# A planned transformer-and-recurrence kernel: other planner prices, a recurrence in 32 chunks of 32 steps, output in 2 KB pieces

## The chip, the cores and the metric

The kernel runs on one core of a Trainium2 chip. The metric is the device time of one execution in microseconds (us), taken as the median of several runs. Engines are named as in the profile: PE is TensorE (matrix products; PEld are its weight loads), ACT is ScalarE (activations), DVE is VectorE, POOL is GpSimd, SP is SyncE, which here only issues transfers.

## The reference

The input x has 8 batch entries of 1024 tokens (64 x 16) with 128 channels, all in fp32. Three things are computed one after the other.

- Layer 0: eight heads of attention with scores over all 1024 tokens of the entry. The exponential of the scores is normalised over one token axis (64 values apart by 16), and the result is put through an exponential once more and normalised over the other axis (16 values). Then come the output product, a residual, a layer norm, a feed-forward part of 512 hidden units with relu, a residual and a layer norm.
- Layer 1, additive attention, with t the tokens and B their layer norm:

```
Wi     = B @ W.T
scores = sum_d v[d] * tanh(Wi[i, d] + Wi[j, d])      # 1024 x 1024 x 128 tanh per entry
t      = t + softmax(scores, axis=j) @ B
```

- Layer 1, recurrence: the layer norm of t times a weight, normalised over all entries and tokens (per channel), and then, from token to token of an entry, with y starting at zero:

```
y = sigmoid(wx[:, token] + y @ V.T);   t[token] += y
```

## The kernel before

**Planned part.** Function `fast_path` first loads weights and multiplies some of them together. Then all work of layer 0 and of the additive attention is put down as a list of operations of a `Plan` (lines 409 to 538): an operation has one engine or a choice of engines with a price in us each, the keys that it reads and writes, and a priority. `Plan.emit` is a list scheduler. It keeps a clock for each engine, takes the engine that can start first, and gives it, among the operations that could start within 0.15 us of that, the one with the best priority. An operation's inputs count as ready at the end of their producer plus that producer's `LATENCY`, or plus `AGAIN` where it ran on the same engine. The order that comes out is the order of the instructions on each engine; at run time each engine goes through its queue in order and waits on semaphores. Prices and latencies thus decide the order and some choices of engine, and nothing else.

Batch entries overlap: layer 0 of entry b + 1 is planned together with the additive attention of entry b. A pair of query tiles in layer 0 goes through scores (PE, L851), exponential (ACT, L854), sums and reciprocal (DVE, L858 and L859), division (DVE, L862), second exponential (ACT, L871), sums and reciprocal (DVE, L874 and L875), division (POOL, L885), transposes through PSUM (PE, L765; DVE, L777), the product with the values (PE, L899) and a sum (DVE, L906). The second attention makes groups of rows, four or more of them. A group is either done wholly on ACT, which adds by its bias (`tanh_row`, L994), or added on DVE (`add_row`, L998, or `add_rows`, L1004) or POOL (`add_rows`, L1004) into one of the `th` slots and put through one tanh on ACT (L1040). PE weighs the rows with v and collects them in the PSUM tile `sa` (L1057), and the slot comes free. Transposes and projections share two PSUM banks; `through_bank` (L755) takes a `Bank` and gives it back.

After the additive attention of an entry its tokens are parked in DRAM (L1205) in halves, and so is their projection wx (L1221).

**Tail.** When the plan is out, its SBUF is given up and the tail begins (lines 1325 to 1389). The statistics are put together, the parked tokens are fetched into `xr` (L1340), and the normalised wx is written as `ws`, one DVE instruction for each step number l (L1346). The recurrence is cut into `NCH` = 64 chunks of `LCH` = 16 tokens, which run side by side. To find each chunk's starting value, a first pass over 16 steps runs on the tokens of the chunk ahead of it, beginning at nothing; the second pass over 16 steps produces the output, so there are 32 steps. A step has two halves, of 32 chunks each and all 8 entries (256 columns): a product of the identity with `ws` (L1365), a product of the weight with the former y on top (L1367), a sigmoid on ACT (L1369), and, in the second pass, a copy on DVE into `ys` (L1374). In the first pass chunk 0 has no predecessor and is left out (`skip`); its y is cleared before the second pass (L1372). At the end 16 pieces of 4 tiles each are transposed (PE, L1382), added to `xr` (DVE, L1384) and sent out (L1386), by turns from the ACT and the SP queue, in rows of 512 B:

```
out=a["out"][b, 4 * g * P : 4 * (g + 1) * P, :].rearrange("(t p) c -> p t c", p=P), in_=ot
```

Of the kernel before, what the change touches and what calls it, by code (L numbers as in the profile page):

```python
# [9 lines left out]
F32 = mybir.dt.float32  # L10
# [388 lines left out]
class Bank:  # L399


    def __init__(self, *choice):
        self.choice = choice

    def __call__(self):
# [3 lines left out]
class Plan:  # L409
# [14 lines left out]

    LATENCY = {"PE": 0.12, "ACT": 0.08, "DVE": 0.08, "POOL": 0.15, "SP": 8.0}
    AGAIN = {"PE": 0.0, "ACT": 0.0, "DVE": 0.04, "POOL": 0.1, "SP": 8.0}

# [27 lines left out]
    def emit(self, slack=0.15, switch=0.1, stay=0.015):  # L455
# [26 lines left out]
        def start_at(n, t, e):  # L482
            take = ops[n][5]
            if take:
                t = max(t, min(bank_free.get(c[0], 0.0) for c in take.choice))
            if e == "POOL" or (e == "DVE" and ops[n][8]):
                t = max(t, port_free)
            return max(t, free[e])
# [20 lines left out]
        while any(open_.values()):  # L509
            first, e = min(  # L510
                (min(start_at(n, t, e) for n, t in open_[e]), i) for i, e in enumerate(engines) if open_[e]
            )
            assert first < never
            e = engines[e]
            n, start = min(
                ((n, s) for n, s in ((n, start_at(n, t, e)) for n, t in open_[e]) if s <= first + slack),
                key=lambda c: (ops[c[0]][2][0] + places[c[0]][e][1] + (stay if e == "PE" and ops[c[0]][3] != mode else 0), c[0]),
            )
            _, fn, _, m, _, take, give, _, port = ops[n]
            if take:  # L520
                take.name, take.tile = min(take.choice, key=lambda c: bank_free.get(c[0], 0.0))
                bank_free[take.name] = never
            cost = places[n][e][0]
            if e == "PE":
                if m != mode:
                    cost += switch
                mode = m
            free[e] = start + (cost if e != "SP" else 0.2)
            if e == "POOL" or (e == "DVE" and port):
                port_free = start + cost  # L530
            began[n], done[n], by[n] = start, start + cost, e
            for q in places[n]:
                open_[q] = [c for c in open_[q] if c[0] != n]
            if give:
                bank_free[give.name] = done[n] + self.LATENCY[e]
            self.order.append((n, e, start, done[n]))
            fn(e)
            finish(n)
# [22 lines left out]
def fast_path(ctx: ExitStack, tc: tile.TileContext, a: dict, fits):  # L561
# [12 lines left out]
    SCALE = 1.0 / math.sqrt(C)  # L574
    NCH = 64
    LCH = N // NCH
# [21 lines left out]

    parked = [tile_of(dram, f"parked{b}", [P, NT, C]) for b in range(NB)]

# [183 lines left out]
    def layer0(b):  # L784
# [16 lines left out]
        for n_part, part in enumerate(parts):  # L801
# [3 lines left out]
            for h in range(H):  # L805
# [18 lines left out]
                for s in () if alone and n_part else range(2):  # L824

                    def values(bank, h=h, s=s):
# [6 lines left out]
                    through_bank(  # L833
                        values, 0.95, [kx], copy(vp[:, 4 * s : 4 * s + 4, :]), evict(0.68), [], [kvp + (s,)], L0, banks
                    )
                for qt in qts:
# [11 lines left out]
                    def scores(_, sc=sc, u=u, qt=qt):  # L848
# [3 lines left out]

                    add(("PE", 1.74), scores, r=[kx, ("u", h % 2, qt // 4)], w=[kc], pri=L0)
                    add(("ACT", 0.98), lambda _, sc=sc: nc.scalar.activation(sc, sc, AF.Exp, scale=SCALE),  # L854
                        r=[kc], w=[kc], pri=L0)
# [7 lines left out]

                    add(("DVE", 1.49), first_sums, r=[kc], w=[k1], pri=L0)
                    add(("DVE", 1.22), divide, r=[kc, k1], w=[ke], pri=L0)
# [4 lines left out]
                    ks = [("e", pair, q) for q in range(2)]  # L870
                    add(("ACT", 1.9), lambda _, e2=e2: nc.scalar.activation(e2, e2, AF.Exp), r=ks, w=ks, pri=L0)  # L871

# [3 lines left out]

                    add(("DVE", 3.25), second_sums, r=ks, w=[k2], pri=L0)
                    na = next_aT()
                    aT = aTs[na]
                    for q in range(2):  # L880
# [7 lines left out]
                        for s in range(2):  # L888
                            through_bank(
                                transposes([e[:, t * P : (t + 1) * P] for t in range(4 * s, 4 * s + 4)]), 0.52, [ke],  # L890
                                copy(aT[:, 4 * s : 4 * s + 4, q * P : (q + 1) * P]), evict(0.68), [],
                                [("aT", na, q, s)], L0, banks,
# [15 lines left out]
                    for s in range(2):  # L908
                        add(
                            ("PE", 1.74), lambda _, attend=attend, s=s: attend(s),  # L910
                            r=[kvp + (p,) for p in range(2)] + [("aT", na, q, p) for q in range(2) for p in range(2)],
# [5 lines left out]
            for qh in range(2) if part is None else (part,):  # L917
                Xg, kg = X[:, 4 * qh : 4 * qh + 4, :], kX + (qh,)
                through_bank(
                    transposes([zs[:, t * P : (t + 1) * P] for t in range(4 * qh, 4 * qh + 4)]), 0.52, [kz + (qh,)],  # L920
                    copy(Xg), evict(0.68), [], [kg], L0, banks,
                )

                def affine1(Xg=Xg):
# [5 lines left out]
                through_bank(  # L930
                    transposes([Xg[:, i, :] for i in range(4)]), 0.52, [kg], copy(z1T), evict(0.68), [], [k1], L0, banks
                )
# [38 lines left out]
    def group(it, at0, r0, k, wiT, all_wi, L1, ROWS, fillers, chain, left, both, first_half):  # L971
# [30 lines left out]
        def add_rows(eng, c):  # L1002
# [8 lines left out]
        work = {  # L1011
            "ACT": [(0.18 + 0.833e-3 * (w - begin[c]), lambda c=c, r=r: tanh_row(c, r)) for c, r in each],
            "POOL": [
                (0.27 + 1.62e-3 * k * (w - begin[c]), lambda c=c: add_rows(nc.gpsimd, c)) for c in range(4)
            ],
            "DVE": [(0.30 + 1.04e-3 * (w - begin[c]), lambda c=c, r=r: add_row(c, r)) for c, r in each]
            if k < 4
# [35 lines left out]
        def times_v(_):  # L1053
# [14 lines left out]
        add(  # L1068
            ("PE", k * (1.69e-3 * (w - begin[0]) + 0.005 * n)), times_v, r=[("tanh", g)] + before,
            w=[("sa", it, r0)] + after, pri=L1, mode="groups", give=slot,  # L1070
# [101 lines left out]
    def attention(b, it, X, kX, B, kB, E_at, L1):  # L1172

        for j0 in range(it + 1, NT, 4):
# [3 lines left out]
                [("E", it, j) for j in js],  # L1178
                copy(ET[:, j0 - 1 : j0 - 1 + len(js), :]), ("DVE", 0.15 + 0.132 * len(js)), [],
                [("ET", j) for j in js], L1,  # L1180
# [19 lines left out]
        if it % 4 != 3:  # L1200
# [3 lines left out]
        add(  # L1204
            ("SP", 4.0), lambda _: nc.sync.dma_start(out=parked[b][:, 4 * qh : 4 * qh + 4, :], in_=Xg),  # L1205
            r=[kg], w=[("parked", b, qh)], pri=L1,
# [129 lines left out]

    ys = rn.tile([P, NB, N], F32, tag="ys", name="ys")
    xr = rn.tile([P, NB, NT, C], F32, tag="xr", name="xr")
    for b in range(NB):
        nc.sync.dma_start(out=xr[:, b], in_=parked[b])  # L1340
    steps = ys.rearrange("p b (c l) -> p c b l", l=LCH)

    ws = rn.tile([P, LCH, NCH, NB], F32, tag="ws", name="ws")
    for l in range(LCH):
        step = wx.rearrange("p b (c l) -> p l c b", l=LCH)[:, l]
        nc.vector.tensor_scalar(ws[:, l], step, sc, off, ALU.mult, ALU.add)  # L1346

    with tc.tile_pool(name="ps_w", bufs=2, space=PSUM) as ps_w, tc.tile_pool(
        name="ps_t", bufs=2, space=PSUM
    ) as ps_t:
        HC = NCH // 2
        prev = [None, None]
        for k in range(2 * LCH):
            l = k % LCH
            early = k < LCH
            for half in range(2):
                c0, c1 = half * HC, (half + 1) * HC  # L1360
                skip = 1 if early and half == 0 else 0
                src = ws[:, l, c0 + skip - early : c1 - early, :]
                acc = ps_w.tile([P, HC, NB], F32, tag=f"acc{half}", name=f"acc{half}")
                to = acc[:, skip:, :]
                nc.tensor.matmul(to, ident, src, start=True, stop=k == 0)  # L1365
                if k:
                    nc.tensor.matmul(to, vf_sb, prev[half][:, skip:, :], start=False, stop=True)  # L1367
                y = rn.tile([P, HC, NB], F32, tag=f"y{half}", name=f"y{half}", bufs=3)
                nc.scalar.activation(y[:, skip:, :], to, AF.Sigmoid)  # L1369
                if k == LCH - 1 and half == 0:  # L1370

                    nc.vector.memset(y[:, 0:1, :], 0.0)  # L1372
                if not early:
                    nc.vector.tensor_copy(steps[:, c0:c1, :, l], y)  # L1374
                prev[half] = y

        n = 0
        for g in range(NT // 4):
            for b in range(NB):
                pt = ps_t.tile([P, 4, C], F32, tag="yt", name="yt")  # L1380
                for i in range(4):
                    nc.tensor.transpose(pt[:, i, :], ys[:, b, (4 * g + i) * P : (4 * g + i + 1) * P], ident)  # L1382
                ot = rn.tile([P, 4, C], F32, tag="ot", name="ot", bufs=3)
                nc.vector.tensor_tensor(ot, pt, xr[:, b, 4 * g : 4 * g + 4, :], ALU.add)  # L1384
                eng = nc.sync if n % 2 else nc.scalar
                eng.dma_start(  # L1386
                    out=a["out"][b, 4 * g * P : 4 * (g + 1) * P, :].rearrange("(t p) c -> p t c", p=P), in_=ot
                )
                n += 1
# [67 lines left out]
```

## Time and profile before

| what | us |
|---|---|
| median of 3 runs (5790.97 to 5795.5) | 5794.7 |
| the profiled execution's own time | 5790.2 |
| its span, first to last instruction | 5788.3 |
| PE busy (modelled) | 5221.0 |
| ACT busy | 5282.6 |
| DVE busy | 4697.6 |
| POOL busy | 4218.7 |
| last instruction of the planned part on PE begins | 5702.9 |
| first product of the recurrence (L1365) | 5709.5 |
| last product of the recurrence (L1367) | 5765.1 |
| last add of the output (L1384) begins | 5782.6 |

Busy times are sums over one profiled execution; engines overlap. A group of the profile gives the source line, engine and operation, what is written from what, the shape and count, then the busy time and the mean of one instruction in ns, and then how long the engine stood idle before them and who released it. The lines of waits give total us, number and longest. The lines of a timeline give start, duration and how many instructions were merged. The clock is that of PE's array, as a share of its full rate. An fp32 product shows as two matmul instructions; a transpose as one.

### The profile page before, as it was taken

The numbers are of one execution on the slowest core, as the hardware profiler recorded it, in microseconds if no ns is written. First come the engines' busy times: TensorE is split into PE (matmuls) and PEld (weight loads), VectorE is DVE, ScalarE is ACT, GpSimd is POOL, SyncE is SP. The second block draws the span as 40 slices with busy tenths as digits, with TensorE's granted clock in tenths as the row PEclk, the third lists the DMA queues.
The fourth block names the chain that finished last, engine by engine and source line by source line (L and its number), as shares of the span: only waits on it lengthen the run. The fifth ranks groups of instructions, "written<-read, shape, count | busy, mean of one in ns | idle before, by whom it ended". The sixth has DMA issues, their size and how long they took to land.

```text
span 5788.3 us, 97417 instructions
## 1 busy us (share of the span) xinstructions
PE 5221.0 (90%) x38885; PEld 2783.0 (48%) x38885; DVE 4697.6 (81%) x7236; ACT 5282.6 (91%) x4978; POOL 4218.7 (73%) x2714
## 2 busy tenths in 40 slices
PE   8899999999889999899998998899998999986567
PEld 6555544555445455454554554444554454443125
DVE  7899766877897788977998788977889678898885
ACT  5489999999999999999998999999998999999993
POOL 2352798788788879798786887788796887863871
PEclk9999999999999999999999999999998999998998
DMA  2000000000000000000000000000000000000001
GB/s 59 1 4 1 1 1 5 7 3 1 1 5 8 1 1 5 5 5 1 1 5 5 5 1 1 5 8 1 1 1 3 6 1 1 1 26 8 1 1 63
DMA packets 27328, 37.79 MB, mean 7 GB/s; under 512 B 2464, under 2 KB 19232, under 8 KB 26864
## 3 DMA queue, kind: packets, MB, share of 16 engines
q1 hardware_dynamic: 21760, 27.99, 1.5%
q8 instruction: 307, 5.03, 0.4%
q10 hardware_dynamic: 4944, 3.16, 0.2%
q14 instruction: 157, 1.29, 0.1%
q0 software_dynamic: 160, 0.33, 0.0%
HBM read 19.41 MB, written 12.06 MB: 5 GB/s over the span
## 4 chain that ended last, share of the span: by engine, by line
PE 52%; DVE 23%; ACT 19%; issue 4%; POOL 2%; DMA 0%; DVEq 0%; ACTq 0%; POOLq 0%; SPq 0%
PE sa L1057 19%; PE m L899 11%; PE sc L851 9%; ACT th L1040 8%; ACT th L994 7%; PE m L765 6%; DVE aT L777 2%; DVE th L1004 2%; DVE th L998 2%; DVE stat_e L874 2%; DVE stat_e L858 2%; ACT wx L871 2%; ACT sc L854 2%; DVE wx L862 2%; DVE X L737 2%
## 5 line engine op out<-in xcount | busy, mean ns | idle before, releaser
L1004 POOL TENSOR_TENSOR th<-wiT 128x1024 f32<-128x1024 f32 (+52 forms) x2124 | 3167.8, 1526 | 405.9 <-PE sa L1057 337.5
L1057 PE MATMUL sa<-th,vpat 128*32 128x512 f32 (+33 forms) x24576 | 2121.8, 470 | 230.9 <-ACT th L1040 219.4
L994 ACT ACTIVATE th<-wiT 128x128 f32<-128x128 f32 (+60 forms) x3092 | 2231.2, 795 | 13.7 <-PE sa L1057 13.5
L1040 ACT ACTIVATE th<-th 128x2490 f32<-128x2490 f32 (+50 forms) x760 | 2069.4, 2745 | 98.9 <-DVE th L998 52.5
L885 POOL TENSOR_TENSOR wx<-wx,stat_e 128x1024 f32<-128x1024 f32 x512 | 992.5, 1959 | 862.2 <-DVE stat_e L875 600.9
L1057 PEld LDWEIGHTS sa<-th,vpat 128*32 128x32 f32 x24576 | 674.8, 112 | 1480.7 <-issue 854.4
L851 PE MATMUL sc<-xT,wx 128*128 128x512 f32 x2048 | 982.2, 604 | 24.8 <-DVE wx L862 23.4
L899 PE MATMUL m<-aT,wx 128*128 128x256 f32 x3584 | 883.1, 394 | 15.1 <-DVE aT L777 13.6
L899 PEld LDWEIGHTS m<-aT,wx 128*128 128x128 f32 x3584 | 668.6, 194 | 269.0 <-issue 112.8
L998 DVE TENSOR_SCALAR_CACHE_REDUCE th<-wiT 128x328 f32<-128x328 f32 (+36 forms) x960 | 681.0, 709 | 83.9 <-PE sa L1057 17.8
L858 DVE TENSOR_REDUCE stat_e<-sc 128x16 f32<-128x1024 f32 x512 | 620.5, 1212 | 154.1 <-ACT sc L854 153.0
L777 DVE COPY aT<-m 128x512 f32<-128x512 f32 x927 | 601.4, 676 | 168.7 <-PE m L765 165.1
L874 DVE TENSOR_REDUCE stat_e<-wx 128x128 f32<-128x2048 f32 x256 | 583.7, 2280 | 129.8 <-ACT wx L871 129.0
L765 PE MATMUL m<-ident,wx 128*128 128x128 f32 x3896 | 573.7, 283 | 80.4 <-DVE aT L777 47.0
L862 DVE TENSOR_TENSOR wx<-sc,stat_e 128x1024 f32<-128x1024 f32 x512 | 623.2, 1218 | 22.9 <-POOL wx L885 0.5
L765 PEld LDWEIGHTS m<-ident,wx 128*128 128x128 f32 x3896 | 432.4, 142 | 378.4 <-issue 175.2
L854 ACT ACTIVATE sc<-sc 128x1024 f32<-128x1024 f32 x512 | 513.4, 1005 | 96.6 <-PE sc L851 83.4
L871 ACT ACTIVATE wx<-wx 128x2048 f32<-128x2048 f32 x256 | 486.8, 1902 | 91.4 <-DVE wx L862 88.2
L851 PEld LDWEIGHTS sc<-xT,wx 128*128 128x128 f32 x2048 | 358.4, 192 | 353.2 <-issue 300.3
L1004 DVE TENSOR_TENSOR th<-wiT 128x1024 f32<-128x1024 f32 (+27 forms) x288 | 361.3, 1302 | 2.0 <-ACT th L994 1.1
L875 DVE RECIPROCAL stat_e<-stat_e 128x128 f32<-128x128 f32 x256 | 244.0, 953 | 8.8
L906 DVE TENSOR_TENSOR zs<-m,zs 128x256 f32<-128x256 f32 x212 | 86.0, 406 | 170.0 <-PE m L899 169.4
(168 smaller groups left out, 3040.6 us busy)
## 6 DMA issues: line engine op xcount, KB each, us to landing
xT<-in_xt_dram SPq DMA_DIRECT2D x8, 512.0 KB, 3.7
th<-in_x_dram SPq DMA_DIRECT2D x8, 512.0 KB, 7.0
parked<-X SPq DMA_DIRECT2D x16, 256.0 KB, 2.0
xr<-parked SPq DMA_DIRECT2D x8, 512.0 KB, 7.0
parked_wx<-bT SPq DMA_DIRECT2D x14, 256.0 KB, 2.0
wx<-parked_wx SPq DMA_DIRECT2D x7, 512.0 KB, 3.3
out_dram<-ot ACTq DMA_DIRECT2D x8, 256.0 KB, 2.4
out_dram<-ot SPq DMA_DIRECT2D x8, 256.0 KB, 2.4
```

Source lines behind the costliest of these rows:

```text
L765: nc.tensor.transpose(bank[:, i * P : (i + 1) * P], s, ident)
L777: nc.vector.tensor_copy(dst, src)
L851: nc.tensor.matmul(sc[:, cols], u[:, qt * P : (qt + 1) * P], xT[:, cols], start=True, stop=True)
L858: nc.vector.tensor_reduce(r1, sc.rearrange("p (m g) -> p g m", g=G), AX.X, ALU.add)
L862: nc.vector.tensor_tensor(e3, sc3, r1.unsqueeze(1).to_broadcast([P, M, G]), ALU.mult)
L885: nc.gpsimd.tensor_tensor(e3, e3, r2[:, q, :].unsqueeze(2).to_broadcast([P, M, G]), ALU.mult)
L899: nc.tensor.matmul(bank()[:, :256], vp[:, t, :], aT[:, t, :], start=t == 0, stop=t == NT - 1)
L994: nc.scalar.activation(rows(c)[:, r, :], wiT[:, i0 + begin[c] :], AF.Tanh, bias=w_i(c, r))
L998: nc.vector.tensor_scalar(rows(c)[:, r, :], wiT[:, i0 + begin[c] :], w_i(c, r), 0.0, ALU.add, ALU.add, accum_out=unused)
L1004: eng.tensor_tensor(rows(c), wiT[:, i0 + begin[c] :].unsqueeze(1).to_broadcast(shape), w_i(c).unsqueeze(2).to_broadcast(shape), ALU.add,)
L1040: lambda _: nc.scalar.activation(slot()[:, : at[4]], slot()[:, : at[4]], AF.Tanh),
L1057: nc.tensor.matmul(sa[32 * c : 32 * c + 32, s:s1], vpat[:, 31 - r0 - r : 63 - r0 - r], rows(c)[:, r, s - at0 - begin[c] : s1 - at0 - begin ...
```

## The change

There are four parts.

1. The planner's `LATENCY` and `AGAIN` get larger values, and prices of single operations change: scores, value products, exponentials, sums and copies are priced higher by 0.01 to 0.11 us, a DVE row lower at its fixed part (0.30 to 0.21), a times-v product at 0.03 instead of 0.005 a piece. The scheduler itself and the priorities stay.
2. `Bank` can hold a choice of its own for an engine (`own`, `of`). No caller gives one.
3. The recurrence: `NCH` is 32 and `LCH` 32. The first pass has `EARLY` = 16 steps, on the last 16 tokens of the chunk ahead, and the second pass 32, so 48 steps. The halves are now of 4 entries with all 32 chunks each (128 columns). `ws` is written in 32 instructions of 256 elements, in the order in which the steps use it. Chunk 0 is left out of the first pass in both halves, and both are cleared.
4. The output: a partition now holds eight consecutive tokens, so `ys` is laid out by token modulo 8, a piece is sent in rows of 2 KB, and the pieces go entry by entry. There are four `ot` buffers and four PSUM tiles for the transposes instead of three and two. The tokens are parked in plain token order, so a parked half is written in rows of 512 B instead of 2 KB; the fetch has 4 KB rows as before.

The diff, cut to its core:

```diff
-    LATENCY = {"PE": 0.12, "ACT": 0.08, "DVE": 0.08, "POOL": 0.15, "SP": 8.0}
-    AGAIN = {"PE": 0.0, "ACT": 0.0, "DVE": 0.04, "POOL": 0.1, "SP": 8.0}
+    LATENCY = {"PE": 0.28, "ACT": 0.2, "DVE": 0.15, "POOL": 0.3, "SP": 8.0}
+    AGAIN = {"PE": 0.0, "ACT": 0.0, "DVE": 0.08, "POOL": 0.15, "SP": 8.0}
...
-                t = max(t, min(bank_free.get(c[0], 0.0) for c in take.choice))
+                t = max(t, min(bank_free.get(c[0], 0.0) for c in take.of(e)))
...
-    NCH = 64
+    NCH = 32
...
-    parked = [tile_of(dram, f"parked{b}", [P, NT, C]) for b in range(NB)]
+    parked = [tile_of(dram, f"parked{b}", [N, C]) for b in range(NB)]
...
-                    add(("PE", 1.74), scores, r=[kx, ("u", h % 2, qt // 4)], w=[kc], pri=L0)
-                    add(("ACT", 0.98), lambda _, sc=sc: nc.scalar.activation(sc, sc, AF.Exp, scale=SCALE),
+                    add(("PE", 1.81), scores, r=[kx, ("u", h % 2, qt // 4)], w=[kc], pri=L0)
+                    add(("ACT", 1.02), lambda _, sc=sc: nc.scalar.activation(sc, sc, AF.Exp, scale=SCALE),
...
-                    add(("DVE", 1.49), first_sums, r=[kc], w=[k1], pri=L0)
+                    add(("DVE", 1.6), first_sums, r=[kc], w=[k1], pri=L0)
...
-            "ACT": [(0.18 + 0.833e-3 * (w - begin[c]), lambda c=c, r=r: tanh_row(c, r)) for c, r in each],
+            "ACT": [(0.19 + 0.833e-3 * (w - begin[c]), lambda c=c, r=r: tanh_row(c, r)) for c, r in each],
...
-            "DVE": [(0.30 + 1.04e-3 * (w - begin[c]), lambda c=c, r=r: add_row(c, r)) for c, r in each]
+            "DVE": [(0.21 + 1.05e-3 * (w - begin[c]), lambda c=c, r=r: add_row(c, r)) for c, r in each]
...
-            ("PE", k * (1.69e-3 * (w - begin[0]) + 0.005 * n)), times_v, r=[("tanh", g)] + before,
+            ("PE", k * (1.67e-3 * (w - begin[0]) + 0.03 * n)), times_v, r=[("tanh", g)] + before,
...
+    EARLY = 16
+    HB = NB // 2
+    ws = rn.tile([P, LCH, NB, NCH], F32, tag="ws", name="ws")
+    ys = rn.tile([P, NB, NT, NCH, LCH // NT], F32, tag="ys", name="ys")
+    steps = wx.rearrange("p b (c l) -> p l b c", l=LCH)
+    order = [LCH - EARLY + k for k in range(EARLY)] + list(range(LCH))
+    for l in order[:LCH]:
+        nc.vector.tensor_scalar(ws[:, l], steps[:, l], sc, off, ALU.mult, ALU.add)
...
+        for k, l in enumerate(order):
+            early = k < EARLY
+            skip = 1 if early else 0
             for half in range(2):
...
+                bs = slice(half * HB, (half + 1) * HB)
+                acc = ps_w.tile([P, HB, NCH], F32, tag=f"acc{half}", name=f"acc{half}")
+                to = acc[:, :, skip:]
+                nc.tensor.matmul(to, ident, ws[:, l, bs, 0 : NCH - skip], start=True, stop=k == 0)
                 if k:
...
+                    nc.tensor.matmul(to, vf_sb, prev[half][:, :, skip:], start=False, stop=True)
+                y = rn.tile([P, HB, NCH], F32, tag=f"y{half}", name=f"y{half}", bufs=3)
+                nc.scalar.activation(y[:, :, skip:], to, AF.Sigmoid)
...
-                    nc.vector.tensor_copy(steps[:, c0:c1, :, l], y)
+                    nc.vector.tensor_copy(ys[:, bs, l % NT, :, l // NT], y)
...
-                    out=a["out"][b, 4 * g * P : 4 * (g + 1) * P, :].rearrange("(t p) c -> p t c", p=P), in_=ot
+                    out=a["out"][b].rearrange("(p t) c -> p t c", t=NT)[:, 4 * g : 4 * g + 4, :], in_=ot
```

## The prediction, made before the result was known

> **What bounds the kernel now.** I read the page first (engines, slices), then the waits of ScalarE (ACT), then the busy time of stretches of the span, then the tail's groups and its timeline. From the page:
>
> ```profile
> span 5788.3 us, 97417 instructions
> PE 5221.0 (90%) x38885; PEld 2783.0 (48%) x38885; DVE 4697.6 (81%) x7236; ACT 5282.6 (91%) x4978; POOL 4218.7 (73%) x2714
> PE   8899999999889999899998998899998999986567
> ACT  5489999999999999999998999999998999999993
> ```
>
> ACT and PE are both busy nine tenths in every slice from the fourth to the thirty-fifth: in the planned part of the kernel these two bound together. The last slice is the tail (recurrence and output), where ACT has 3. Busy time by stretch, two batches in the middle and three stretches of the tail (us; then busy and count of PE, PEld, DVE, ACT, POOL; then TensorE clock, DMA share, GB/s):
>
> ```profile
> 1800.00:2470.00 670.00, 630.81 (x4831) 333.07 (x4827) 548.21 (x826) 638.93 (x556) 543.10 (x350) 0.98 0.01 3
> 2470.00:3130.00 660.00, 618.65 (x4696) 324.12 (x4695) 557.23 (x826) 621.71 (x534) 531.00 (x337) 0.98 0.01 4
> 5709.00:5713.00 4.00, 3.48 (x8) 2.86 (x9) 4.00 (x7) 1.93 (x3) 0.00 (x0) 0.50 1.01 398
> 5741.00:5766.50 25.50, 25.44 (x121) 22.20 (x120) 12.53 (x31) 11.24 (x30) 0.00 (x0) 1.00 0.00 1
> 5766.50:5788.30 21.80, 11.79 (x60) 7.87 (x58) 10.96 (x17) 0.00 (x0) 0.00 (x0) 0.77 0.69 196
> ```
>
> ACT idles 5% in the middle batches; the recurrence is all PE (25.44 of 25.50); the output stage is no engine's. Its groups:
>
> ```profile
> L1365 PE MATMUL acc<-ws,ident 128*128 128x256 f32 x96 | 29.5, 390 | 0.0
> L1369 ACT ACTIVATE y<-acc 128x256 f32<-128x256 f32 x48 | 18.4, 383 | 22.2 <-PE acc L1367 11.1 <-DVE ys L1374 11.0
> L1346 DVE TENSOR_SCALAR ws<-wx,scb,offb 128x512 f32<-128x512 f32 x16 | 11.1, 839 | 0.1
> L1384 DVE TENSOR_TENSOR ot<-yt,xr 128x512 f32<-128x512 f32 x16 | 11.0, 691 | 5.8 <-DMA out_dram<-ot 5.2 <-PE yt L1382 0.7
> ```
>
> The output adds wait 5.2 us for output transfers, because the three ot buffers are still being written out. The rest of the working rests on these lines of the timeline (start, length):
>
> ```profile
> 5695.00 1.95 PE L1186 MATMUL m<-B,E 128*128 128x129 f32 x16
> 5713.01 1.30 PE L1367 MATMUL acc<-y,vf_sb 128*128 128x248 f32 x4
> 5757.80 0.60 PE L1365 MATMUL acc<-ws,ident 128*128 128x256 f32 x2
> 5758.23 0.59 PE L1367 MATMUL acc<-y,vf_sb 128*128 128x256 f32 x2
> 5765.14 0.59 PE L1367 MATMUL acc<-y,vf_sb 128*128 128x256 f32 x2
> 5782.62 0.69 DVE L1384 TENSOR_TENSOR ot<-yt,xr 128x512 f32<-128x512 f32 x1 [0.68 <-DMA out_dram<-ot]
> ```
>
> and these of ACT's waits:
>
> ```profile
> ACT wx L871 <- DVE wx L862: 88.2, 50, 14.4
> ACT sc L854 <- PE sc L851: 83.4, 71, 6.0
> ACT th L1040 <- DVE th L998: 52.5, 31, 4.7
> ACT th L1040 <- DVE th L1004: 36.3, 21, 4.0
> ```
>
> and two of the page's groups, ACT rows and POOL rows of the tanh work:
>
> ```profile
> L1004 POOL TENSOR_TENSOR th<-wiT 128x1024 f32<-128x1024 f32 (+52 forms) x2124 | 3167.8, 1526 | 405.9 <-PE sa L1057 337.5
> L994 ACT ACTIVATE th<-wiT 128x128 f32<-128x128 f32 (+60 forms) x3092 | 2231.2, 795 | 13.7 <-PE sa L1057 13.5
> ```
>
> **What the Trainium skill says.** "TensorE: Matmul & The Clock Gate", Back-to-back issue gap, gives N/2.4 + 2.5 ns a matmul: 0.109 us for 256 columns. The trace disagrees for this fp32 form: 0.43 us for two (5757.80 to 5758.23), 0.215 each. I use the trace. The same page, What's actually happening, says that the array runs at half rate until about 3.4 us of activity; the trace agrees (clock 0.50 in 5709 to 5713, 1.00 from 5713.6 by the clock records). "DMA: Bandwidth & Descriptors", Why small descriptors are slow, says each packet carries a fixed cost; the trace agrees: packet records last 28.6 ns for the 512 B of the output and 84 ns for the 2 KB of the parked writes, so 16 engines carry 286 and 390 GB/s.
>
> **The change, part by part.**
>
> *Recurrence.* Before, 32 steps, each two halves of two products of 256 columns, two instructions a product: 8 x 0.215 = 1.72 us. From the first recurrent product (5713.01) to the last (5765.14): 52.1 us. After, 16 early and 32 late steps, halves of 128 columns (4 batches x 32 chunks). PE's spacing at this width: sixteen matmuls of 129 columns span 1.95 us, one alone lasts 0.275, so (1.95 - 0.275)/15 = 0.112 us; a step is 8 x 0.112 = 0.89 us. The chain through one half is the other limit: 0.112 + 0.275 for the product, 0.04 to ACT (5738.97 to 5739.01 in the records), a sigmoid of 128 elements (0.383 for 256, 1.007 for 1024, L854: slope 0.81 ns, so 0.28), about 0.04 back, and a weight load of about 0.11 ahead of the product, since the wait sits on the load: 0.86 us. So PE still ends last, narrowly: 47 steps x 0.90 = 42.3 us. The start is earlier: the first normalisation has 256 elements instead of 512 (0.15 + 1.04 ns each: 0.42 against 0.68), the first product is half as wide at the cold clock (0.21 instead of 0.41 us an instruction), and fewer cold products stand ahead of the first recurrent one: 5711.7 against 5713.0, -1.3 us. Against that, PE idles while the sigmoid table loads (1.28 us, at 5710.76 now), so it may stay at half rate one window longer: +1.7 us. Sum: 42.3 - 52.1 - 1.3 + 1.7 = -9.4 us; bounds -11 (warm at once) and 0 (a step of 1.09 us: another 0.2 us in the chain).
>
> *Normalisation and copies on DVE.* 32 x 0.42 = 13.4 us instead of 11.1, but a step needs one only each 0.9 us, and the first late copy comes after 16 steps, so it hides behind the recurrence. 64 copies of 128 elements (0.28 us) instead of 32 of 256 (0.42): 18 us in the 29 us of the late steps, hidden too. The second clearing of the first chunk is 0.07 us of DVE, ahead of its use. Uncovered, these would be 2.3, 4.5 and 0.1 us.
>
> *Output.* Now from the last recurrent product (5765.14) to the last add's end (5783.31) is 18.2 us. After: last copy 1.1 us behind the last product (shorter product, sigmoid, copy; 1.5 now), then 16 adds. With 2 KB packets 256 KB take 0.67 us, below the add's 0.69, and there are four ot and four PSUM buffers; so DVE paces it, 16 x 0.75 with its hand-over = 12.0, or PE's transposes where the clock is at half (4 x 0.22 = 0.9 a piece). I take 12.5: 13.6 us, -4.6; bounds -5.5 and -1. The last transfer lands in 2.0 us (parked, 2 KB) rather than 2.4 (out): -0.4.
>
> *Parked writes.* 16 writes now go in 512 B pieces: 256 KB in 0.92 instead of 0.67 us of the queues, at a DMA share of 0.01 to 0.02. Nothing waits for them until the reload at 5705.1; the last is issued at 5697.6, lands about 2.0 us later and then about 2.3. Cost 0; uncovered, 0.3.
>
> Tail together: -9.4 - 4.6 - 0.4 = -14.4; I take -13.5, a rounding towards the losses of hand-overs not seen.
>
> *The planner.* `own` is passed by no caller: nothing. The prices and latencies change the order of instructions on each engine up to 5700 us, not the work as such, apart from which engine adds rows. PE's prices rise by about 4% for scores and attend, ACT's by 1 to 4%, POOL's not at all; DVE's rise by 0.11 (first sums), 0.05 and 0.02, and fall by 0.09 for an added row. The trace's reading of these: first exponential 1.007 (0.98 to 1.02), first sums with reciprocal 1.215 + 0.253 = 1.47 (1.49 to 1.6), a row of 535 elements comes every 0.93 us on DVE (5655.06, 5655.99, 5656.92; before's price 0.86, after's 0.77), PE's result reaches ACT about 0.2 us after its priced end (a tail of 0.17 behind the last spacing, and 0.04; 0.12 to 0.28). So before's prices lie closer, after's are mostly cautious and one is too low. The trace cannot say what order results. What it gives is the scatter: the xT loads, one a batch, are issued at 955.0, 1640.7, 2307.8, 2983.3, 3668.6, apart by 685.7, 667.1, 675.5, 685.2 under one set of prices, a deviation of 9 us. Over seven batches and two schedules that is 9 x 2.65 x 1.41 = 34 us; milestones within a batch jitter and partly cancel, so I estimate 15 to 30. My likeliest value is 0.
>
> Sum on the profiled run (span 5788.3, time 5790.2): 5776.7. The median of the runs is 4.5 above that run: **5781**.
>
> **Rivals.** *B, caution covers waits.* The four waits shown are 260 us of ACT, in which the planner thought an input ready that was not. With latencies 0.07 to 0.16 longer it puts a row of tanh there instead. For: ACT bounds, and these waits are frequent and short (173, 1.5 us each). Against: much of such a wait is a late chain and not a hand-over, and PE is as full as ACT. If 15% go: -40, 5741.
>
> *C, rows move to ACT.* A group of four rows is either added on POOL or DVE and put through one tanh of ACT, or done on ACT in four (L994). By the records an L994 costs ACT 0.19 us beside its elements (0.284 less an overlap of 0.096), the single tanh 0.10: a group that moves to ACT costs the bound engine 4 x 0.19 - 0.10 = 0.65 us. Place: batches 1 to 6. With slots priced free 0.28 us after PE instead of 0.12 and POOL's hand-over at 0.30 instead of 0.15, the planner finds ACT free first more often. For: POOL already idles 337.5 us for slots that PE holds. Against: ACT's own prices rise, DVE's row gets cheaper. It decides from (13.5 + 11.6) / 0.65 = 39 groups, 5% of the 760 that go through one tanh now. At 9%, 68 x 0.65 = 44 us, or for any order as much worse: 5825. The cheap DVE row is a smaller case of the same sign: 353 rows in the last batch (5220 to 5677), each priced 0.085 us lower, are at most 30 us of work that the plan does not see, the first part of it free, as ACT waits for these rows only 12.4 us there.
>
> *D, the recurrence becomes a chain.* If a step is 1.05 instead of 0.90 us, 7 us of the gain are lost: 5788. It lies inside the likeliest case. That the change does nothing it says is excluded: widths and packet sizes are in the code.
>
> **How the numbers follow.** A (tail gain, planned part within 13 us of now): 0.45, 5781, own range 5768 to 5794. B: 0.30, 5741, reaching from 5710 to 5768. C and other worse orders: 0.25, 5825, from 5794 to 5855. 0.2% of 5794.7 is 11.6 us, about what a measurement here can tell from no change: bounds 5783.1 and 5806.3. Faster: 0.27 of A and all of B, 0.57; same: 0.18 of A and 0.05 of C, 0.23; slower 0.20. The range leaves a third of B below 5738 and some 0.1 of C above 5822.
>
> **What would show it.** Right: the recurrence's matmuls of 128 columns at 0.11 us, a step of 0.9, last add some 14 us after the last recurrent product without waits for output transfers, the tail after the last projection 13 us shorter; the four waits of ACT summing to about 260 again. B: that sum clearly under 220. C: over 3250 of the L994 (3092 now, four to eight a group), or ACT waiting for DVE rows over 35 us after 5220. Wrong altogether: the span up to the tail moved by more than 45 us either way, or a step above 1.1 us.

## The result and the profile after

The changed kernel takes 5802.0 us (median, 5797.8 to 5808.4) against 5791.9 us for the kernel before in the same comparison: ratio 1.0016, 95% interval 1.0009 to 1.0023. It is slower by a sixth of a per cent, where 0.24% faster was forecast. The new tail gives nearly what was expected of it, and the planned part takes more than that back.

The page of the changed kernel; line numbers are higher by 5 to 7 in the planned part and by up to 14 in the tail:

```profile
span 5799.4 us, 97823 instructions
PE 5211.0 (90%) x39013; PEld 2774.9 (48%) x39013; DVE 4749.4 (82%) x7487; ACT 5268.3 (91%) x4948; POOL 4210.9 (73%) x2702
PE   8899999899998999999998999989998998997567
ACT  5489999999997999999999999979998799999994
```

Both kernels end the planned part with the same stretch of work, which begins with an exponential of 640 columns into E. By the timelines, before and then after:

```profile
5677.07 0.70 ACT L1153 ACTIVATE E<-sa 128x640 f32<-128x640 f32 x1 [2.07 <-PE sa L1057]
5702.32 0.70 ACT L1158 ACTIVATE E<-sa 128x640 f32<-128x640 f32 x1 [2.07 <-PE sa L1062]
```

So the planned part is 25.3 us longer. From there to the end it is 111.2 us before and 97.0 after: the tail is 14.2 us shorter. 25.3 - 14.2 = 11.1, the difference of the spans (5799.4 - 5788.3).

The middle batches (same stretches and columns as before) show no engine that became the bound; ACT is busy 6 us less in the first and 29 us more in the second of them, so work has shifted between stretches:

```profile
1800.00:2470.00 670.00, 628.14 (x4705) 328.60 (x4707) 560.13 (x798) 633.00 (x537) 547.52 (x346) 0.97 0.01 3
2470.00:3130.00 660.00, 631.02 (x4836) 328.57 (x4825) 544.96 (x823) 651.15 (x589) 551.54 (x350) 1.00 0.01 4
```

The four waits of ACT that the prediction added up:

```profile
ACT sc L859 <- PE sc L856: 133.1, 60, 15.4
ACT wx L876 <- DVE wx L867: 79.7, 31, 16.1
ACT th L1045 <- DVE th L1003: 50.4, 39, 5.5
ACT th L1045 <- DVE th L1009: 31.1, 21, 3.8
```

They come to 294 us, 260 before: the wait for scores grew by 50 us and the others shrank by 16 together. And the two groups of rows:

```profile
L1009 POOL TENSOR_TENSOR th<-wiT 128x848 f32<-128x848 f32 (+53 forms) x2112 | 3156.9, 1530 | 411.6 <-PE sa L1062 352.6
L999 ACT ACTIVATE th<-wiT 128x504 f32<-128x504 f32 (+51 forms) x3020 | 2202.4, 802 | 44.6 <-PE sa L1062 27.1
```

ACT adds fewer rows itself (3020 instead of 3092), the opposite of what rival C had named.

The tail, first a stretch within the recurrence, then the output (same columns as before):

```profile
5755.00:5775.00 20.00, 20.00 (x182) 20.00 (x181) 12.68 (x46) 12.45 (x45) 0.00 (x0) 1.00 0.00 1
5783.00:5799.40 16.40, 7.05 (x49) 4.83 (x46) 9.20 (x15) 0.00 (x0) 0.00 (x0) 0.81 0.71 260
```

its groups:

```profile
L1372 PE MATMUL acc<-ws,ident 128*128 128x128 f32 x128 | 24.8, 275 | 0.0
L1376 ACT ACTIVATE y<-acc 128x128 f32<-128x128 f32 x64 | 17.8, 278 | 10.8 <-PE acc L1374 10.8
L1360 DVE TENSOR_SCALAR ws<-wx,scb,offb 128x256 f32<-128x256 f32 x32 | 14.1, 534 | 0.1
L1392 DVE TENSOR_TENSOR ot<-yt,xr 128x512 f32<-128x512 f32 x16 | 10.4, 687 | 1.2 <-DMA out_dram<-ot 1.0
```

and its timeline:

```profile
5737.26 1.22 PE L1374 MATMUL acc<-y,vf_sb 128*128 128x124 f32 x4 [0.41 <-ACT y L1376]
...
5780.43 0.39 PE L1374 MATMUL acc<-y,vf_sb 128*128 128x128 f32 x2
...
5780.88 0.39 PE L1374 MATMUL acc<-y,vf_sb 128*128 128x128 f32 x2
...
5787.78 5.67 DVE L1392 TENSOR_TENSOR ot<-yt,xr 128x512 f32<-128x512 f32 x8 [0.40 <-DMA out_dram<-ot]
```

PE is still busy throughout the recurrence (20.00 of 20.00). A half step takes 0.45 us (5780.43 to 5780.88), a step 0.89. The output adds wait 1.0 us for transfers instead of 5.2, and the last eight follow one another without a gap.

### The profile page after: what moved, and what is told of

It is laid out like the page before. It is cut to its first block, busy times and chain, and to the rows that moved or that the text cites. A ratio compares the mean times of both kernels' runs of the same rounds, so it can differ in the third digit from the quotient of the medians.

```text
span 5799.4 us, 97823 instructions
## 1 busy us (share of the span) xinstructions
PE 5211.0 (90%) x39013; PEld 2774.9 (48%) x39013; DVE 4749.4 (82%) x7487; ACT 5268.3 (91%) x4948; POOL 4210.9 (73%) x2702
## 3 DMA queue, kind: packets, MB, share of 16 engines
q10 hardware_dynamic: 1872, 3.16, 0.2%
## 4 chain that ended last, share of the span: by engine, by line
PE 43%; DVE 26%; ACT 25%; issue 5%; POOL 1%; DMA 0%; DVEq 0%; ACTq 0%; POOLq 0%; SPq 0%
PE sa L1062 16%; ACT th L1045 10%; ACT th L999 10%; PE sc L856 8%; PE m L904 8%; PE m L770 4%; DVE th L1003 4%; DVE th L1009 3%; DVE stat_e L879 3%; DVE aT L782 3%; ACT sc L859 2%; DVE stat_e L863 2%; ACT wx L876 2%; DVE wx L867 2%; PE m L834 1%
## 5 line engine op out<-in xcount | busy, mean ns | idle before, releaser
L1009 POOL TENSOR_TENSOR th<-wiT 128x848 f32<-128x848 f32 (+53 forms) x2112 | 3156.9, 1530 | 411.6 <-PE sa L1062 352.6
L1062 PE MATMUL sa<-th,vpat 128*32 128x512 f32 (+35 forms) x24576 | 2120.6, 468 | 246.5 <-ACT th L1045 236.6
L999 ACT ACTIVATE th<-wiT 128x504 f32<-128x504 f32 (+51 forms) x3020 | 2202.4, 802 | 44.6 <-PE sa L1062 27.1
L1045 ACT ACTIVATE th<-th 128x2292 f32<-128x2292 f32 (+50 forms) x768 | 2083.9, 2738 | 94.1 <-DVE th L1003 50.4
L856 PE MATMUL sc<-xT,wx 128*128 128x512 f32 x2048 | 994.8, 611 | 38.9 <-DVE wx L867 37.1
L904 PE MATMUL m<-aT,wx 128*128 128x256 f32 x3584 | 863.3, 388 | 9.4 <-DVE aT L782 8.2
L1003 DVE TENSOR_SCALAR_CACHE_REDUCE th<-wiT 128x384 f32<-128x384 f32 (+52 forms) x1068 | 741.8, 695 | 86.0 <-PE sa L1062 15.1
L904 PEld LDWEIGHTS m<-aT,wx 128*128 128x128 f32 x3584 | 658.6, 191 | 245.9 <-issue 97.5
L782 DVE COPY aT<-m 128x512 f32<-128x512 f32 x922 | 595.5, 673 | 143.1 <-PE m L770 141.2
L867 DVE TENSOR_TENSOR wx<-sc,stat_e 128x1024 f32<-128x1024 f32 x512 | 623.5, 1218 | 23.7 <-PE m L770 0.3
L1009 DVE TENSOR_TENSOR th<-wiT 128x1024 f32<-128x1024 f32 (+29 forms) x276 | 403.2, 1505 | 4.2 <-PE sa L1062 4.2
L738 POOL TENSOR_TENSOR stat<-stat,neg_half 128x4 f32<-128x4 f32 x64 | 65.7, 1027 | 254.4 <-DVE stat L735 244.0
```

What stands on the lines that cost most here:

```text
L782: nc.vector.tensor_copy(dst, src)
L856: nc.tensor.matmul(sc[:, cols], u[:, qt * P : (qt + 1) * P], xT[:, cols], start=True, stop=True)
L867: nc.vector.tensor_tensor(e3, sc3, r1.unsqueeze(1).to_broadcast([P, M, G]), ALU.mult)
L904: nc.tensor.matmul(bank()[:, :256], vp[:, t, :], aT[:, t, :], start=t == 0, stop=t == NT - 1)
L999: nc.scalar.activation(rows(c)[:, r, :], wiT[:, i0 + begin[c] :], AF.Tanh, bias=w_i(c, r))
L1003: nc.vector.tensor_scalar(rows(c)[:, r, :], wiT[:, i0 + begin[c] :], w_i(c, r), 0.0, ALU.add, ALU.add, accum_out=unused)
```

## The experiments

Three theories stood against one another for the 25.3 us. *Luck*: the order that comes out of the planner is one draw out of many, and any other set of numbers draws again. *Caution* or *prices*: the new latencies, or the new prices, make worse orders as such, whatever the draw. *Tail*: the tail acts back on the planned part through the parked writes. Planned part means, in all that follows, the time up to that exponential of 640 columns, in the one profiled execution; before it is 5677.1 us and after 5702.3 us. One execution can differ from the median of its kernel by some us (at most 4.8 in the runs below, for the new numbers with 0.14).

### The two halves of the change, and the two halves of the planner's numbers

`tail_only` keeps the prices and latencies of the kernel before and takes all else. `plan_only` has the new prices and latencies with all else as before. `tail_lat` and `tail_price` are the changed kernel with one of the two set back:

```diff
 # tail_price: latencies set back (tail_lat: the prices instead)
-    LATENCY = {"PE": 0.28, "ACT": 0.2, "DVE": 0.15, "POOL": 0.3, "SP": 8.0}
-    AGAIN = {"PE": 0.0, "ACT": 0.0, "DVE": 0.08, "POOL": 0.15, "SP": 8.0}
+    LATENCY = {"PE": 0.12, "ACT": 0.08, "DVE": 0.08, "POOL": 0.15, "SP": 8.0}
+    AGAIN = {"PE": 0.0, "ACT": 0.0, "DVE": 0.04, "POOL": 0.1, "SP": 8.0}
```

Expected of `tail_only`:

> The new recurrence, output and parking with the former prices and latencies of the kernel before. If the two parts add up, the planned part ends as in the kernel before (the 640-wide exponential of E at 5677 us of the span, within 2 us) and the span falls by 14.4 us to about 5774; ratio to before 0.9975. If the tail acts back on the planned part (through the parked writes in 512 B pieces), the planned part ends more than 5 us later and the gain is lost.

Of `plan_only`:

> The new prices and latencies with the old recurrence and output. Parts add up: the planned part is 25 us longer, as in the changed kernel, the tail 111 us as before; span about 5814, ratio 1.0044. If the parked writes cost something in the planned part, it is under 20 us longer.

Of `tail_lat`:

> The new tail with only the latencies changed, prices as before. Theory of luck (any other order is a draw with a deviation of 10 to 30 us): the planned part lies anywhere from 30 us shorter to 30 us longer, and not at the sum of parts. Rival, caution costs: it carries most of the 25 us, planned part 15 to 25 us longer. Rival, cheap DVE row costs: 0 to 5 us longer.

Of `tail_price`:

> The new tail with only the prices changed, latencies as before. Luck: anywhere from 30 us shorter to 30 us longer, and the two halves do not add up to 25. Rival, prices cost (a DVE row priced 0.09 us too low, ACT waits for rows): 15 to 25 us longer, with ACT waiting for DVE rows more than the 52 us of before. Rival, caution in the latencies costs: 0 to 5 us longer.

Measured (time is the median; the ratio is to the kernel before, run beside it):

| kernel | time, us | ratio (95%) | planned part, us | from there to the end, us |
|---|---|---|---|---|
| `tail_only` | 5776.6 | 0.9974 (0.9965 to 0.9984) | 5676.9 | 96.0 |
| `plan_only` | 5822.1 | 1.0058 (1.0044 to 1.0071) | 5705.7 | 112.5 |
| `tail_lat` | 5783.5 | 0.9987 (0.9980 to 0.9993) | 5687.9 | 97.0 |
| `tail_price` | 5850.2 | 1.0100 (1.0084 to 1.0115) | 5751.2 | 97.5 |

The tail is settled: with the former planner's numbers the planned part ends where it did (5676.9 against 5677.1), so the parked writes cost it nothing, and the time falls by 14.8 us. The planner's numbers alone cost 30.7 us. The two come to +15.9, while the changed kernel, in a comparison of its own, is 10.2 above before; of the 5.7 between, the profile puts 3.4 in the planned part of `plan_only` and 1.3 in its tail. The 3.4 are there when the second batch of layer 0 begins (its first exponential at 410.9 us, 407.5 in the changed kernel) and stay the same from there on; why stays open.

The halves of the planner's numbers do not add up at all: latencies alone +11 us, prices alone +74, both +25. That speaks for luck, but 74 us was outside the 30 us that the theory had named. The rivals missed both sizes too: caution had 15 to 25 us for the latencies, prices had 15 to 25 us for the prices, with ACT waiting more than 52 us for DVE rows, and it waited 47.6.

### The same numbers, another draw

`emit` looks 0.15 us ahead for operations with a better priority. 0.14 or 0.16 instead favours nothing, but changes which of two is taken here and there. Two runs have the former numbers, two the new, all with the new tail:

```diff
-    def emit(self, slack=0.15, switch=0.1, stay=0.015):
+    def emit(self, slack=0.14, switch=0.1, stay=0.015):
```

Expected of `old_slack14`:

> New tail, former prices and latencies of the kernel before; the planner looks 0.14 us ahead instead of 0.15, a change that favours nothing. Theory of luck (each order is a draw with a deviation of 20 to 40 us about one mean for all prices): the planned part ends 20 to 40 us away from the 5677 us of before, most likely later, as before would be a lucky draw. Theory of a price (before's prices give good orders, the new ones bad ones): within 10 us of 5677.

Of `old_slack16`:

> The same with 0.16 us. Luck: 20 to 40 us away from 5677, in either direction. Price: within 10 us of 5677.

Of `new_slack14`:

> The changed kernel, 0.14 us ahead instead of 0.15. Luck: 20 to 40 us away from the 5702 us at which its planned part ends, as often below as above. Price: within 10 us of 5702, and above both runs with the prices of before.

Of `new_slack16`:

> The same with 0.16 us. Luck: 20 to 40 us away from 5702. Price: within 10 us of 5702, and above both runs with the prices of before.

Measured, beside the orders already known. ACT's busy and idle time, rows and the start of the third batch are counted in the trace's records: busy is time in activation instructions, rows are the additions that ACT does by its bias from 410 to 600 us, and a batch starts with the first exponential of its layer 0.

| order | time, us | ratio (95%) | planned part, us | ACT busy + idle in it, us | ACT rows, 410 to 600 | third batch from, us |
|---|---|---|---|---|---|---|
| former, 0.14 | 5757.1 | 0.9935 (0.9916 to 0.9955) | 5658.8 | 5254.7 + 404.2 | 313 | 1010.2 |
| former, 0.15 (`tail_only`) | 5776.6 | 0.9974 | 5676.9 | 5257.9 + 419.0 | 321 | 1004.1 |
| former, 0.16 | 5824.3 | 1.0051 (1.0032 to 1.0071) | 5724.9 | 5247.4 + 477.4 | 221 | 1046.3 |
| new, 0.14 | 5786.2 | 0.9990 (0.9982 to 0.9997) | 5682.8 | 5225.7 + 457.2 | 310 | 1011.1 |
| new, 0.15 (the change) | 5802.0 | 1.0016 | 5702.3 | 5237.8 + 464.5 | 293 | 1013.9 |
| new, 0.16 | 5774.1 | 0.9966 (0.9955 to 0.9977) | 5676.9 | 5224.5 + 452.4 | 234 | 1030.7 |
| new latencies only | 5783.5 | 0.9987 | 5687.9 | 5258.5 + 429.4 | 292 | 1020.6 |
| new prices only | 5850.2 | 1.0100 | 5751.2 | 5228.8 + 522.4 | 158 | 1053.1 |

A hundredth of a microsecond of look-ahead moves the end by 18 to 48 us. The theory of a price allowed 10 us and fails in all four runs. Luck had named 20 to 40 us: two runs stayed just under it (18.1 and 19.5) and one went over it, and the first came out earlier where later was thought most likely.

The three orders with the former numbers have a mean of 5686.9 us, the three with the new ones 5687.3 (by the medians of their times 5786.0 and 5787.4). All eight have a mean of 5695 and a deviation of 30. So neither set is shown to be better than the other, and at 0.16 us the new numbers win by 48 us where at 0.15 they lose by 25. What is shown is that a neutral redraw moves the end by as much as the step from before to after. That the new numbers cost nothing on average is not shown: with a deviation of 30 us the mean of three is uncertain by 17 us and the difference of two such means by 24, as much as the step itself.

The new numbers do have an effect of their own that holds in each pair of the same look-ahead: ACT is less busy by 20 to 29 us, as more rows go to DVE (1056 to 1068 single rows against 956 to 996). What decides is ACT's idle time, which varies by 118 us over the eight orders, its busy time by 34.

*A better version.* `old_slack14`, the new tail with the former numbers and 0.14 us, takes 5757.1 us: 0.65% below the kernel before and 45 us below the changed one. It is the best of eight draws, chosen after they were measured.

### Where a bad draw loses

The table's last two columns go together: the fewer rows ACT adds from 410 to 600 us, the later the third batch starts (correlation -0.97 over the eight). In that stretch the planner lays the narrow rows of the first batch (tiles 4 to 7) beside layer 0 of the second batch, and may give them to DVE or ACT, those of tile 4 to POOL too. The correlation alone proves little: an order that is late for any reason has fewer rows done by 600 us. The stretch in `tail_only`:

```profile
410.00:600.00 190.00, 182.23 (x1315) 111.20 (x1313) 176.33 (x256) 182.03 (x374) 54.11 (x30) 0.98 0.00 1
```

and in `tail_price`, with ACT's longest wait there under it:

```profile
410.00:600.00 190.00, 165.16 (x974) 102.20 (x972) 171.37 (x279) 127.42 (x209) 65.60 (x38) 0.95 0.00 1
```

```profile
ACT sc L859 <- PE sc L856: 51.1, 13, 10.0
```

In `tail_only` PE, DVE and ACT (the first, third and fourth pair) are all nearly full. In `tail_price` DVE is the fullest with 171 of 190 us, and ACT is busy 127 instead of 182. DVE adds 32 rows of its kind (L1003) there instead of 11, and POOL makes 11 additions instead of one. ACT waits 51.1 us for scores, 4.6 in `tail_only`. The explanation to be tested: each row on DVE delays DVE's work for layer 0, so PE's scores come late, and ACT, which has been given fewer rows, waits for them. The test allows these groups ACT alone, or DVE alone:

```diff
+                    if b == 0 and not wide:
+                        fillers = [("ACT", 0.1)]    # old_dve0: ("DVE", 0.1)
                     todo.append((r0 + 0.5 * (not wide), it, 0 if it == pair[0] else N - pair[0] * P, r0, k, fillers))
```

Expected of `price_act0`:

> New tail, new prices, former latencies (the slowest order, planned part to 5751 us, third batch of layer 0 from 1053 us); the narrow groups of rows of the first batch (tiles 4 to 7) may go to ACT alone. Theory of place (DVE is full from 410 to 600 us, so a row put there stalls layer 0, and ACT with it): ACT busy over 175 of those 190 us instead of 127, third batch from 1000 to 1015 us, 40 to 50 us earlier, and planned part shorter by 20 to 70 us, as the order after it is drawn anew. Rival (the loss is spread, the rows are a symptom): third batch within 15 us of 1053.

Of `old16_act0`:

> The same edit in the kernel with the former prices and latencies that looks 0.16 us ahead (third batch from 1046 us, planned part to 5725 us). Place: ACT busy over 175 of the 190 us from 410 to 600 instead of 142, third batch from 1000 to 1015 us. Rival: within 15 us of 1046.

Of `new_act0`:

> The same edit in the changed kernel (third batch from 1014 us, planned part to 5702 us, ACT busy 170 of the 190 us). Place: little left to gain there, third batch from 1000 to 1012 us; the end 30 us to either side of 5702, by luck.

Of `old_dve0`:

> The reverse in the kernel with the new tail and the former prices and latencies (third batch from 1004 us): these groups may go to DVE alone. Place: ACT busy under 130 of the 190 us, third batch from 1050 us or later. Rival: within 15 us of 1004.

The stretch in `price_act0`:

```profile
410.00:600.00 190.00, 178.43 (x1350) 108.27 (x1349) 160.13 (x227) 187.16 (x409) 52.54 (x29) 1.00 0.01 1
```

and in `old_dve0`:

```profile
410.00:600.00 190.00, 141.04 (x621) 83.56 (x619) 178.55 (x316) 69.57 (x45) 41.82 (x23) 0.87 0.00 1
```

| kernel | time, us | ratio (95%) | ACT busy, 410 to 600 | third batch from (unedited) | planned part (unedited) |
|---|---|---|---|---|---|
| `price_act0` | 5807.0 | 1.0025 (1.0014 to 1.0036) | 187.2 | 1007.9 (1053.1) | 5708.8 (5751.2) |
| `old16_act0` | 5789.3 | 0.9995 (0.9986 to 1.0005) | 182.5 | 1010.5 (1046.3) | 5692.6 (5724.9) |
| `new_act0` | 5794.3 | 0.9999 (0.9990 to 1.0008) | 184.1 | 1006.8 (1013.9) | 5696.1 (5702.3) |
| `old_dve0` | 6001.5 | 1.0364 (1.0343 to 1.0384) | 69.6 | 1231.8 (1004.1) | 5903.0 (5676.9) |

The place holds in all four. With ACT alone all three orders start the third batch within 4 us of one another, wherever they started it before; with DVE alone 228 us are lost by then, and DVE is the fullest engine (179 of 190 us, PE 141, ACT 70). What is won or lost here stays: at the start of each later batch and at the end, `price_act0` is 41 to 46 us ahead of its unedited order, `old16_act0` 30 to 36, `new_act0` 5 to 8, and `old_dve0` 223 to 228 us behind. So the edit does not draw the later order anew, as the expectation of `price_act0` had it. The edits to ACT take the rows from POOL too, but in the unedited order of `old16_act0` POOL adds none in this stretch, so there the 36 us are due to the rows on DVE.

How a row on DVE costs so much is not shown. In `tail_price` the rows take 9 us more of DVE in this stretch than in `tail_only` (18.7 against 10.2 us, both kinds), and the third batch starts 49 us later; the new numbers with 0.16 us put more on it (26.7 us) and start only 27 us later. PE's own waits for DVE there come to 15.5 us in `tail_price`, 13.8 of them for the copies that empty the PSUM banks (L782) and 1.7 for the division that frees a score tile (L867).

Of `tail_price`'s 74 us, 45 were lost here (1053.1 against 1007.9); of the changed kernel's 25, 7 to 10 (1013.9 against 1006.8 and, in `tail_only`, 1004.1). This part may be the prices' doing and not luck: at each look-ahead the new numbers put more rows on DVE in this stretch (24 against 16, 24 against 11, 44 against 32). But the third batch then starts 0.9 us later, 9.8 later and 15.6 earlier, which does not decide it.

From the third batch on, the eight orders take 4671 us with a deviation of 18; this remainder has no single place that a run here has shown. Against `tail_only` the changed kernel is 9.8 us late at the third batch, 21.5 at the fifth, 2.0 at the seventh and 25.6 at the last exponential of layer 0: time is lost and won back on the way, and most of the difference that remains arises in the last two batches. New prices with the former latencies are slow behind the third batch in both runs (4698 us, and 4701 in `price_act0`). The two are not independent, as they share the later order, and whether that is a trait of this pairing stays open.

## Why the prediction was wrong, by its own steps

*Recurrence: right.* From the first recurrent product to the last it takes 43.6 us (5737.26 to 5780.88). The prediction had 42.3 and 1.7 for a longer cold clock: 44.0. The step is 0.89 us, PE-bound at 0.112 a matmul as read from 16 matmuls of 129 columns. The cold window came as feared: the clock records have 0.50 until 5741.9, 4.6 us into the recurrence and 7.1 us after its first product; before, it was 4.1 us after the first product (5709.5 to 5713.6). The start moved by 1.3 us, as worked out: from the first normalisation to the first recurrent product 4.46 us before, 3.16 after. The chain through a half was left with little room, so D did not come: at full clock the weight load that waits for a sigmoid starts 0.083 us after the sigmoid's end, and at the first recurrent product, where PE stood idle for it, 0.05, so some 0.03 us of each step were to spare. The sigmoid's 0.278 us at 128 columns and the table load of 1.28 us are close to what the Trainium skill's "ScalarE: Activation LUTs", What ACT_TABLE_LOAD costs, states (186 ns + 0.833 ns an element with an immediate bias, an estimate of 0.293 us; about 1283 ns).

*Output: right, distributed otherwise.* From the last recurrent product to the end of the last add 12.6 us, where 13.6 were forecast and 18.2 stood before. What follows the last add is 5.9 us instead of 5.0, a loss of 0.9, where a gain of 0.4 was forecast: the last transfer lands 3.8 us after its issue instead of 3.0, behind three others that land 0.6 us apart. DVE is no longer held back by transfers, so the transfers trail it. Together -4.7 against -5.0.

*Parked writes, copies, normalisation: right.* They land in 2.3 us instead of 2.0, and nothing waits: the planned part of `tail_only` ends 0.2 us earlier than before. The sum for the tail, -14.4, was measured as -14.2 in the changed kernel's profile, and as -14.8 in the times of `tail_only`. The rounding to -13.5 had no ground.

*The planner: the step that failed is "My likeliest value is 0".* This term of the sum measured +25.3 us. With it the sum closes: 5790.2 - 14.2 + 25.3 = 5801.3, and the profiled execution took 5801.2. (The 4.5 us from that execution to the median came from three runs; over nineteen it is 1.7.) The scatter was estimated from the batches' spacing as 15 to 30 us, and over eight orders it is 30, so a difference of 25 is an ordinary one. But it was used only to widen the range; the centre was set at no change, and nothing in the trace spoke for that. With a scatter twice the tail's gain the sign of the sum could hardly be told. The order of the kernel before is rather a good draw: it ends at 5677, the mean of the eight is 5695 and that of the six with a whole set of numbers 5687, each uncertain by some 11 us. So a redraw from it lost 10 to 18 us on average by these runs, and with that in place of 0 the sum would have been 5791 to 5799, within 5 us of no change. These means are known only from the runs; the trace of before does not give them.

*A reading.* PE and ACT are not "busy nine tenths in every slice": PE's row has seven 8s from the fourth slice to the thirty-fifth, ACT's has two. That both bound the planned part does not hang on it.

*B* had ACT's waits falling by 40 us; they rose by 34 in the changed kernel and by 2 with the latencies alone (110.0, 82.1, 36.8 and 33.8 us). *C* had the sign of the planned part right and the mechanism wrong: 3020 rows on ACT and not over 3250. The price of a DVE row, named there as the smaller case, was placed in the last batch, where it cost nothing (ACT waits for DVE rows 14.5 us there, 12.4 before, and the planned part is 26.3 us late at the last exponential of layer 0 and 25.3 at its end). A place where it does cost is the first 200 us of the second batch.

## What to carry to other kernels

An order from a list scheduler is a draw: here a nudge that favours nothing moved the end by 18 to 48 us, in either direction, where the careful gain in the tail was 14. So cost such an edit at the mean of several draws and not at zero, and before crediting prices with a result, redraw with a neutral nudge. A kernel whose order was kept because it was fast may well have a lucky one; these eight draws fit that, but do not prove it. The time lost by a bad draw can sit in a stretch whose fullest engine is not that of the rest of the kernel: compare milestones between two traces, find the stretch where they part, and tie down the choice that the scheduler has there.

## What the runs showed that was not expected

- A neutral change of 0.01 us in look-ahead moved the end by -18 and +48 us with the one set of numbers, by -20 and -25 with the other.
- 45 us won by the start of the third batch, by taking one choice from the scheduler, were still 42 us at the end of the planned part (`price_act0`).
- Giving the narrow rows of one batch to DVE, the fullest engine of just that stretch, cost 228 us (`old_dve0`), although DVE is idle for nearly a fifth of the span as a whole.
- The packets of the output carry more at 2 KB in the profile too: 260 GB/s at a DMA share of 0.71 in the output stretch, 196 at 0.69 before, which by division is 366 and 284 GB/s at a full share.
